# First attention of a two-layer network: scores computed once, kept in SBUF and shifted there

## The chip, the cores and the metric

The kernel runs on one core of a Trainium2 chip. Its time is the device time of one execution in microseconds (us), the median of three runs. Times of stages and instructions come from one profiled execution of the same program.

## The reference, cut to what matters

Eight batches go through two layers, each a cross attention and a feed-forward part, always on the layer-normalised sum so far. The part that the change touches is the first attention:

```python
# per batch: x 512 x 256, context 1024 x 192, 16 heads of 64
q = layernorm(x) @ w_q;  k, v = split(context @ w_kv)
scores = einsum('bhqd,bhkd->bhqk', q, k) * 64 ** -0.5
out = einsum('bhqk,bhkd->bhqd', softmax(scores), v)
x = x + out @ w_out + b_out
```

After it come, for each batch, two of eight expert networks picked by the batch's first row (`experts`), and a second attention with 16 heads of width 16 (`second_attention`). The last feed-forward part, whose inputs and hidden values are rounded to levels that depend on all eight batches, runs when everything else is done.

## The kernel before

Everything is float32, and softmax's maxima are exact. Heads go in pairs: a pair's two heads of width 64 fill the 128 rows of the array, one in each half. There are 64 pairs in all (eight batches of eight), numbered n; keys go in eight tiles of 128, numbered kt, and the 512 queries lie along the free dimension.

For pair n the first attention does the following.

- `queries(n)`, `keys(n)`: two projections, copied to SBUF by ScalarE. `values` makes the values of four heads at once.
- `maxima(n, i)`: eight score tiles laid out queries by keys are computed for the maxima alone (`sm`, L557), and VectorE reduces each straight from PSUM (`mx`, L564).
- `maxima_rows`: the 512 maxima per head are transposed to rows (`tm`, L576), split in a high and a low part by ScalarE and VectorE (`mr`, L580 and L581), and written into the tile `m_rows` by four small DMAs on SP's queue (L584).
- `scores(n, kt)` through `exponentials`: the scores are computed again, keys by queries (L595), a matmul of `m_ones` with `m_rows` subtracts the maxima within the same PSUM accumulation (L598), and ScalarE takes the exponential from PSUM to SBUF (`e`, L600). GpSimd adds the eight tiles of exponentials up (`esum`, L754 and L756).
- `attend(n, half)`: values times exponentials, in two halves of four tiles (`av`, L696). `normalise` makes the sums over keys by a matmul (`den`, L715), and GpSimd divides by Newton steps (L729 to L737). `project` multiplies by `w_out` and adds to x.

The order on TensorE is written by `weave`. It takes two generators, `first_stream` (the first attention of all batches, then the rest of the last batch) and `second_stream` (for each other batch experts, second attention, last norm), and picks the next step by a planner's account: each step carries its costs on TensorE, on one of the four PSUM slots, and on an engine. A batch's second stream can start only when its first attention is done. TensorE's queue keeps that order; the other engines' queues are ordered by the framework's own scheduler. [...] Every PSUM tile, of both streams, comes from one ring of four slots (`ps_s`), so a tile has to be drained before the fourth one after it can be written.

The weights of the first attention lie whole in SBUF (`wq`, `wkv`, `wo`), and wide tiles of both streams share one ring of 13.

Of the kernel before, what the change touches and what calls it, by code (L numbers as in the profile page):

```python
# [18 lines left out]
P = 128  # L19
# [110 lines left out]
def kernel(  # L130
# [33 lines left out]
    H = 16  # L164
# [7 lines left out]
    NF = FF // P  # L172
    assert S == 512 and D == 256 and L == 1024 and AD == 64 and CD == 16 and NE == 8
# [28 lines left out]

    fold = const.tile([P, AD], F32, name="fold")
# [17 lines left out]
    pp = attn.enter_context(tc.tile_pool(name="pp", bufs=13))  # L221
    op = attn.enter_context(tc.tile_pool(name="op", bufs=2))

    def load_ctx(b):
        raws = []
        for g in range(NK // 4):
            t = pp.tile([P, 4, DC], F32, tag="e", name=f"ctx_{b}_{g}")
            nc.sync.dma_start(
                out=t, in_=cross[b, g * 512 : (g + 1) * 512].rearrange("(t p) d -> p t d", p=P)
            )  # L230
            raws.append(t)
        return raws

    load_x(0)
    loaded = {0: load_ctx(0)}

    wq = wts.tile([P, DH, H * AD], F32, name="wq")
    nc.sync.dma_start(out=wq, in_=a_wq.rearrange("(c p) n -> p c n", p=P))

    wkv = wts.tile([P, 2, 2 * H * AD], F32, name="wkv")  # L240
    nc.sync.dma_start(out=wkv[:, 0, :], in_=a_wkv[0:P, :])
    for h in range(2):
        nc.sync.dma_start(out=wkv[h * CR : (h + 1) * CR, 1, :], in_=a_wkv[P:DC, :])
    wo = wts.tile([P, H // 2, D], F32, name="wo")
    nc.sync.dma_start(out=wo, in_=a_wo.rearrange("(h p) n -> p h n", p=P))
# [96 lines left out]
    def feed_forward_weights():  # L342

        nw, no, wT = (
            [pp.tile([P, 1024], F32, tag="e", name=f"{name}{i}") for i in range(2)]
            for name in ("nw", "no_f", "wT")
# [3 lines left out]
        for i in range(2):  # L350
            nc.sync.dma_start(
                out=no[i].rearrange("p (f n) -> p f n", n=D),
                in_=f_wo[i * 512 : (i + 1) * 512, :].rearrange("(f p) n -> p f n", p=P),
            )
        bir = small.tile([NF, P], F32, tag="bir", name="bir", bufs=1)
# [16 lines left out]
        for k, parts in enumerate((wT, no)):  # L372
# [26 lines left out]
            if k == 0:  # L399
                wi = pp.tile([P, DH, FF], BF16, tag="e", name="wi")  # L400
# [38 lines left out]
    def normed(pool, tag, b, mean, rs):  # L439
        xn = pool.tile([P, NT, D], F32, tag=tag, name=f"xn_{b}")  # L440
        for t in range(NT):
            nc.gpsimd.tensor_scalar(  # L442
                xn[:, t, :], xs[b][:, t, :], mean(t), rs(t), ALU.subtract, ALU.mult
            )
        return xn
# [18 lines left out]
    def layernorm_T(b, xT, by_place=False):  # L464
# [3 lines left out]
        def norm():  # L468
            mv, rs = norm_of(b)
            xn.append(  # L470
                normed(pp, "e", b, lambda t: mv[:, t, 0:1], lambda t: rs[:, t : t + 1])
            )
# [10 lines left out]
    def context_T(b, raws, c1, c2):  # L483

        def wide(g):
# [16 lines left out]
        for g in range(NK // 4):  # L504
            steps.append((0, [(0.5, "s", "act", 0.6, "full")], lambda g=g: wide(g)))
            steps.append((0, [(0.5, "s", "dve", 0.5, "full")], lambda g=g: narrow(g)))
# [84 lines left out]
    def exponentials(name, q, k, rows_of, kt, scale):  # L591
# [7 lines left out]
        e = pp.tile([P, 2, 512], F32, tag="e", name=f"e_{name}_{kt}")  # L599
# [6 lines left out]
    def prologue(b):  # L606

        if b in loaded:
            raws = loaded.pop(b)
        else:  # L610
            load_x(b)
            raws = load_ctx(b)
# [9 lines left out]
        return layernorm_T(b, xTs[b]) + context_T(b, raws, c1, c2), bias  # L622

    def first_attention():


        q, k, v, o, mx, es, esum, division = {}, {}, {}, {}, {}, {}, {}, {}
        last = B * NP - 1

        def queries(n):  # L630
            b, p = divmod(n, NP)
            q[n] = kvp.tile([P, S], F32, tag="q", name=f"q_{n}")
            t = bank(f"pq_{n}")
            for c in range(DH):
                nc.tensor.matmul(  # L635
                    t, wq[:, c, tok(p)], xTs[b][:, c, :], start=(c == 0), stop=(c == DH - 1)
# [3 lines left out]
        def keys(n):  # L640
            b, p = divmod(n, NP)
            c1, c2 = contexts[b]
            k[n] = kvp.tile([P, L], F32, tag="k", name=f"k_{n}")
# [6 lines left out]
                        wkv[:, 0, tok(p)],  # L650
                        c1[:, g * 512 : (g + 1) * 512],
                        wkv[g * CR : (g + 1) * CR, 1, tok(p)],
# [7 lines left out]
        def values(m, half):  # L660

            b, g = divmod(m, H // G)
            c1, c2 = contexts[b]
            if half == 0:
                v[m] = kvp.tile([P, NK, G * AD], F32, tag="v", name=f"v_{m}")
            cols = slice(H * AD + g * G * AD, H * AD + (g + 1) * G * AD)
            t = ps_s.tile([P, 2, 512], F32, tag="s", name=f"pv_{m}_{half}")
            parts = []
            for j in range(2):
                for i in range(2):  # L670
# [7 lines left out]
                            wkv[:, 0, cols],  # L678
                            c2[rows_, at],
                            wkv[rows_, 1, cols],  # L680
# [28 lines left out]
        def normalise(n, piece):  # L709


            if piece == 0:
                den = bank(f"den_{n}")
                for h in range(2):
                    nc.tensor.matmul(  # L715
                        den[h * AD : (h + 1) * AD, :],
                        ones_c,
                        esum[n][:, h, :],
# [3 lines left out]
                e = op.tile([P, S], F32, tag="rec", name=f"rec_{n}", bufs=1)  # L722
                y = op.tile([P, S], F32, tag="guess", name=f"guess_{n}", bufs=1)
                division[n] = e, y
                nc.scalar.copy(e, den)
                nc.vector.tensor_scalar(
# [720 lines left out]
```

## Time and profile before

| | |
|---|---|
| median of 3 runs (lowest, highest) | 3667.57 us (3667.2, 3667.66) |
| profiled execution | 3661.27 us, span 3659.5 us |
| TensorE busy, share of the span | 3425.3 us, 94% |
| GpSimd | 2228.9 us, 61% |
| VectorE | 1871.2 us, 51% |
| ScalarE | 1581.8 us, 43% |
| first and last cast of a pair's maxima (`mr`, L580) | 41.2 us, 3132.9 us |
| eight pairs in the steady part (casts of pairs 16 and 24) | 747.1 to 1160.9 us |

The span runs from the first to the last instruction. In the profile's lines an operation is named by its line, engine and tiles, output first; L595 is line 595 of the kernel. PE is TensorE, PEld its weight loads, DVE is VectorE, ACT is ScalarE, POOL is GpSimd, SPq the queue of the sync engine that issues the DMAs. A matmul in float32 appears as two records, and matmuls in different quarters of the array overlap, so that the steps of the chain of waits, not the mean of a record, tell what a tile costs. PEclk is the clock that TensorE was granted, 1.00 being full speed.

### The profile page before, as it was taken

Reading aid. Unit: us, or ns where it says so; the run is one execution under the profiler, and the core shown is the slowest. Engines: PE = TensorE matmul, PEld = TensorE weight load, DVE = VectorE, ACT = ScalarE, POOL = GpSimd, SP = SyncE. Lnnn points to the kernel's source line nnn. Section 1 sums busy time; section 2 is a strip of 40 time slices with the busy share of each in tenths; the row PEclk is TensorE's granted clock in tenths of the full one; section 3 lists DMA queues with packets and bytes.
Section 4 is the critical chain, followed back from the end, with each engine's and each line's share of the span. In section 5 each row is a group of like instructions: output and inputs, shape, how many; then the busy total and the mean of one; then the engine's idle time right before and its main releaser. Section 6 shows DMA issues by size and latency. Waiting matters only on the chain.

```text
span 3659.5 us, 45327 instructions
## 1 busy us (share of the span) xinstructions
PE 3425.3 (94%) x17437; PEld 1636.1 (45%) x17445; DVE 1871.2 (51%) x2327; ACT 1581.8 (43%) x1871; POOL 2228.9 (61%) x1900
## 2 busy tenths in 40 slices
PE   8999999999999999999999999999999999787777
PEld 4444444444444444444444444444444444343336
DVE  4333465544654465544654465544654444355578
ACT  2333244443544344443544344443544334334467
POOL 3888845686556854687556854687456866720012
PEclk9999999999999999999999999999999999998889
DMA  3000110001110111001110010001100000021122
GB/s 103 12 15 1 32 26 20 18 27 27 27 27 1 32 30 27 19 21 29 31 27 1 27 36 21 24 13 33 28 21 15 27 23 13 11 57 38 27 75 75
DMA packets 69395, 102.27 MB, mean 28 GB/s; under 512 B 16815, under 2 KB 48316, under 8 KB 68796
## 3 DMA queue, kind: packets, MB, share of 16 engines
q1 hardware_dynamic: 69180, 99.37, 9.9%
q8 instruction: 139, 2.28, 0.3%
q14 instruction: 76, 0.62, 0.1%
HBM read 37.98 MB, written 9.96 MB: 13 GB/s over the span
## 4 chain that ended last, share of the span: by engine, by line
PE 75%; POOL 11%; DVE 8%; ACT 2%; issue 2%; SPq 1%; DMA 1%; POOLq 0%; ACTq 0%; DVEq 0%
PE av L696 11%; PE s L595 10%; PE sm L557 10%; PE cav L1062 5%; PE acc L519 4%; DVE cmx L564 3%; PE pq L635 3%; PE s_c L595 3%; PE pk L545 3%; POOL esum L756 3%; PE pv L545 3%; PE s L598 3%; POOL xn L442 2%; PE s_c L598 2%; PE sm_c L557 2%
## 5 line engine op out<-in xcount | busy, mean ns | idle before, releaser
L564 DVE TENSOR_REDUCE mx<-sm 128x2 f32<-128x1024 f32 x512 | 626.8, 1225 | 652.5 <-PE sm L557 650.6
L756 POOL TENSOR_TENSOR esum<-esum,e 128x1024 f32<-128x1024 f32 x384 | 905.7, 2358 | 33.5 <-ACT e L600 15.5
L600 ACT ACTIVATE e<-s 128x1024 f32<-128x1024 f32 x512 | 523.5, 1026 | 498.4 <-PE s L598 493.6
L564 DVE TENSOR_REDUCE cmx<-sm_c 128x2 f32<-128x1024 f32 x512 | 607.4, 1217 | 235.1 <-PE sm_c L557 234.5
L754 POOL TENSOR_TENSOR esum<-e,e 128x1024 f32<-128x1024 f32 x64 | 151.2, 2363 | 869.6 <-PE den L715 826.9
L600 ACT ACTIVATE e_c<-s_c 128x1024 f32<-128x1024 f32 x512 | 509.3, 1024 | 276.2 <-PE s_c L598 264.8
L595 PE MATMUL s<-q,k 64*128 64x512 f32 x2048 | 551.4, 615 | 17.9 <-DVE cmx L564 7.2
L557 PE MATMUL sm<-k,q 64*128 64x512 f32 x2048 | 529.8, 595 | 6.0 <-DVE cmx L564 1.9
L696 PE MATMUL av<-e,v 128*64 128x512 f32 x2048 | 467.4, 598 | 0.2 <-ACT k L658 0.2
L598 PE MATMUL s<-m_rows,m_ones 64*128 64x512 f32 x1024 | 414.0, 802 | 0.0
L736 POOL TENSOR_SCALAR guess<-rec 128x512 f32<-128x512 f32 x192 | 286.5, 1492 | 16.6
L595 PE MATMUL s_c<-cq,ck 64*128 64x512 f32 x1024 | 284.1, 548 | 9.5 <-ACT e_c L600 6.3
L595 PEld LDWEIGHTS s<-q,k 64*128 64x128 f32 x2048 | 182.4, 188 | 226.0 <-issue 153.0
L557 PE MATMUL sm_c<-ck,cq 64*128 64x512 f32 x1024 | 221.9, 435 | 57.5 <-DMA ck<-ckl 32.7
L557 PEld LDWEIGHTS sm<-k,q 64*128 64x128 f32 x2048 | 197.6, 188 | 157.3 <-issue 80.1
L696 PEld LDWEIGHTS av<-e,v 128*64 128x64 f32 x2048 | 136.2, 136 | 270.9 <-issue 257.4
L737 POOL TENSOR_TENSOR o<-o,guess 128x512 f32<-128x512 f32 x192 | 244.3, 1273 | 11.1
L684 ACT COPY v<-pv 128x1024 f32<-128x1024 f32 x64 | 64.8, 1013 | 427.3 <-PE pv L547 427.3
L1062 PE MATMUL cav<-e_c,cv 128*32 128x512 f32 x1792 | 218.0, 604 | 0.4 <-ACT e_c L600 0.4
L598 PE MATMUL s_c<-m_rows,m_ones 64*128 64x512 f32 x1024 | 210.4, 401 | 2.9 <-DMA m_rows<-mr_c 2.7
L420 POOL TENSOR_SCALAR ve<-mv 128x4 f32<-128x4 f32 x32 | 7.3, 228 | 297.9 <-DVE mv L418 293.0
L595 PEld LDWEIGHTS s_c<-cq,ck 64*128 64x128 f32 x1024 | 100.4, 190 | 189.5 <-issue 99.5
(219 smaller groups left out, 4317.9 us busy)
## 6 DMA issues: line engine op xcount, KB each, us to landing
cq<-cqs SPq DMA_DIRECT2D x256, 64.0 KB
ck<-ckh SPq DMA_DIRECT2D x128, 128.0 KB
ck<-ckl SPq DMA_DIRECT2D x128, 128.0 KB
w<-in_L_ffn_W_dram SPq DMA_DIRECT2D x32, 256.0 KB
x<-xd SPq DMA_DIRECT2D x16, 512.0 KB
ctx<-in_ctx_dram SPq DMA_DIRECT2D x16, 384.0 KB
x<-in_x_dram SPq DMA_DIRECT2D x8, 512.0 KB
m_rows<-mr SPq DMA_DIRECT2D x256, 2.0 KB
```

The lines of the kernel that those rows point to most:

```text
L545: nc.tensor.matmul(out, lhs, rhs, start=first, stop=False, skip_group_check=True)
L557: nc.tensor.matmul(s[:, h, :], q[half, tok(i)], k[half, g * 512 : (g + 1) * 512], start=True, stop=True,)
L564: nc.vector.tensor_reduce(mx[:, :, i, g], s, AX.X, ALU.max)
L595: nc.tensor.matmul(s[:, h, :], k[half, tok(kt)], q[half, :], start=True, stop=False)
L598: nc.tensor.matmul(s[:, h, :], m_ones[half, :], rows_of[half, :], start=False, stop=True)
L600: nc.scalar.activation(e, s, AF.Exp, scale=scale)
L696: nc.tensor.matmul(av[h * AD : (h + 1) * AD, :], v[m][:, kt, (at + h) * AD : (at + h + 1) * AD], es[n, kt][:, h, :], start=(kt == kts[0]), ...
L736: nc.gpsimd.tensor_scalar(y, e, 1.0, None, ALU.add)
L737: nc.gpsimd.tensor_tensor(o[n], o[n], y, ALU.mult)
L754: nc.gpsimd.tensor_tensor(esum[n], es[n, 0], es[n, 1], ALU.add)
L756: nc.gpsimd.tensor_tensor(esum[n], esum[n], es[n, kt], ALU.add)
L1062: nc.tensor.matmul(av[col : col + SL, :], va[:, v : v + SL], es[p, kt][:, h, :], start=(i == 0), stop=(i == NK // 4 - 1),)
```

## The change

Scores are computed once, keys by queries, and copied to SBUF without the maxima subtracted. VectorE keeps a running maximum over the eight tiles; eight transposes by TensorE and one reduction turn it into the maxima per query. These are spread over all partitions by one pair of matmuls, and added (with a minus sign) to the score tiles in SBUF, two tiles of a pair by VectorE from PSUM, six by GpSimd from a copy. ScalarE then takes the exponential in place. Scores of pair n + 1 are made while pair n is exponentiated. The division is a reciprocal of 256 columns on VectorE, spread by matmuls, and one product on VectorE. The first attention's weights are loaded four heads at a time, and the wide tiles have rings of their own: 12 for the first attention's scores, 5 for the second's exponentials, 3 and 1 for others. `q`, `k` and `v` of the first attention have one buffer each.

```diff
+    RINGS = {"e": 12, "ec": 5, "t": 3, "p": 1}
...
+    def load_weights(m, keys=("q", "kv", "o")):
+        g = m % (H // G)
+        cols = slice(g * G * AD, (g + 1) * G * AD)
+        if "q" in keys:
+            t = wts.tile([P, DH, G * AD], F32, tag="wq", name=f"wq_{m}")
+            nc.sync.dma_start(out=t, in_=a_wq[:, cols].rearrange("(c p) n -> p c n", p=P))
+            weights["q"] = t
...
+        def sums(n):
+            den = bank(f"den_{n}")
+            for h in range(2):
+                for g in range(NT):
                     nc.tensor.matmul(
+                        den[32 * g : 32 * (g + 1), tok(h)],
+                        ones[:, 0:32],
+                        esum[n][:, h, tok(g)],
                         start=True,
                         stop=True,
                     )
+            rec[n] = op.tile([P, 2, P], F32, tag="rec", name=f"rec_{n}", bufs=1)
+            nc.vector.reciprocal(rec[n].rearrange("p h n -> p (h n)"), den[:, : 2 * P])
+
+        def normalise(n):
+            t = bank(f"rb_{n}")
+            for g in range(NT):
+                for h in range(2):
+                    nc.tensor.matmul(
+                        t[h * AD : (h + 1) * AD, tok(g)],
+                        pick[:, g, :],
+                        rec[n][:, h, :],
+                        start=True,
+                        stop=True,
+                    )
+            nc.vector.tensor_tensor(o[n], t, o[n], ALU.mult)
...
         def scores(n, kt):
+            s = ps_s.tile([P, 2, 512], F32, tag="s", name=f"s_{n}_{kt}")
+            for h in range(2):
+                half = slice(h * AD, (h + 1) * AD)
+                nc.tensor.matmul(
+                    s[:, h, :], k[n][half, tok(kt)], q[n][half, :], start=True, stop=True
+                )
+            es[n, kt] = wide("e", [P, 2, 512], f"e_{n}_{kt}")
+            nc.scalar.copy(es[n, kt], s)
+            if kt == 1:
+                run[n] = pp.tile([P, 2, 512], F32, tag="wide", name=f"run_{n}", bufs=2)
+                nc.vector.tensor_tensor(run[n], s, es[n, 0], ALU.max)
+            elif kt > 1:
+                nc.vector.tensor_tensor(run[n], s, run[n], ALU.max)
+
+        def maxima(n):
+            t = ps_s.tile([P, 2, NT, P], F32, tag="s", name=f"trun_{n}")
+            for h in range(2):
+                for i in range(NT):
+                    nc.tensor.transpose(t[:, h, i, :], run[n][:, h, tok(i)], ident)
+            m = small.tile([P, 2, NT], F32, tag="m", name=f"m_{n}", bufs=2)
+            nc.vector.tensor_reduce(m, t, AX.X, ALU.max)
+            return m
+
+        def subtract(n, kt):
+            if kt < 2:
+                nc.vector.tensor_tensor(es[n, kt], mb[n][0], es[n, kt], ALU.add)
+            else:
+                nc.gpsimd.tensor_tensor(es[n, kt], mb[n][1], es[n, kt], ALU.add)
+
+        def spread(n):
+            t = ps_s.tile([P, 2, 512], F32, tag="s", name=f"mb_{n}")
+            for h in range(2):
+                half = slice(h * AD, (h + 1) * AD)
+                nc.tensor.matmul(
+                    t[:, h, :], m_ones[half, :], m_rows[0][half, :], start=True, stop=True
+                )
+            u = pp.tile([P, 2, 512], F32, tag="wide", name=f"mbs_{n}", bufs=2)
+            mb[n] = t, u
+            nc.scalar.copy(u, t)
+            for kt in range(4):
+                subtract(n, kt)
+
+        def exponentiate(n, kt):
+            nc.scalar.activation(es[n, kt], es[n, kt], AF.Exp, scale=AD**-0.5)
...
+            yield 0, SPREAD
+            spread(n)
+            for kt in range(2):
+                exponentiate(n, kt)
             for kt in range(NK):
...
+                    scores(n + 1, kt)
+                if kt + 2 < NK:
+                    exponentiate(n, kt + 2)
+                if kt == 0 and n > 0:
+                    yield 0, SUMS
+                    sums(n - 1)
+                add_up(n, kt)
+                if 1 <= kt <= 4:
+                    subtract(n, kt + 3)
+                if kt == 2 and n > 0:
+                    yield 0, NORM
+                    normalise(n - 1)
+                if kt == 3:
                     yield 0, HALF[0]
                     attend(n, 0)
...
+            yield 0, HALF[1]
+            attend(n, 1)
             if n < last:
+                yield 0, TURN
+                mm = maxima(n + 1)
             if n + 2 <= last:
+                yield from both(n + 2)
             if n < last:
+                yield 0, ROWS
+                maxima_rows(f"{n + 1}", mm, m_rows[0])
             if p % 2 == 0 and n > 0:
                 yield 0, OUT
                 project(n // 2 - 1)
+                load_weights(n // 2, ("o",))
...
+            if p % 2 == 1 and n < last:
+                yield from both_values(n // 2 + 1)
+                if n + 3 <= last:
+                    load_weights(n // 2 + 2, ("q", "kv"))
```

`queries`, `keys`, `values`, `attend`, `maxima_rows` and the second stream's arithmetic stay as they are; `add_up` is the former sum over the eight tiles, on GpSimd as before.

## The prediction, on record before the run

> **What bounds the kernel now.** I read the page's busy times first, then its slices, then a table of stretches.
>
> ```profile
> PE 3425.3 (94%) x17437; PEld 1636.1 (45%) x17445; DVE 1871.2 (51%) x2327; ACT 1581.8 (43%) x1871; POOL 2228.9 (61%) x1900
> ...
> PE   8999999999999999999999999999999999787777
> ...
> PEclk9999999999999999999999999999999999998889
> ```
> ```profile
> 1561.00:1948.00 387.00, 376.28 (x1925) 174.26 (x1922) 201.37 (x246) 169.85 (x199) 262.29 (x224) 1.00 0.10 26
> 3190.00:3440.00 250.00, 194.56 (x1061) 96.08 (x1061) 142.24 (x194) 105.75 (x122) 30.04 (x68) 0.87 0.17 43
> ```
>
> TensorE is busy 97% of a steady stretch at full clock; nothing else is above 68%. The second line is the stage after the first attention: busy 78%, granted clock 0.87. Then come the groups that the change touches, and rows that price new work:
>
> ```profile
> L564 DVE TENSOR_REDUCE mx<-sm 128x2 f32<-128x1024 f32 x512 | 626.8, 1225 | 652.5 <-PE sm L557 650.6
> L756 POOL TENSOR_TENSOR esum<-esum,e 128x1024 f32<-128x1024 f32 x384 | 905.7, 2358 | 33.5 <-ACT e L600 15.5
> L600 ACT ACTIVATE e<-s 128x1024 f32<-128x1024 f32 x512 | 523.5, 1026 | 498.4 <-PE s L598 493.6
> L754 POOL TENSOR_TENSOR esum<-e,e 128x1024 f32<-128x1024 f32 x64 | 151.2, 2363 | 869.6 <-PE den L715 826.9
> L1370 ACT ACTIVATE h<-h,unround 128x1024 f32<-128x1024 f32 x32 | 35.6, 1137 | 8.4 <-DVE h L1367 8.4
> L1086 DVE RECIPROCAL crec<-co 128x16 f32<-128x16 f32 x32 | 8.1, 253 | 1.0
> ```
> ```profile
> 1564.38 0.89 PE s L595 x4
> 1565.50 0.86 PE sm L557 x4
> ...
> 1582.19 1.85 PE cav L1062 x16
> ...
> 1599.63 3.43 PE av L696 x16
> ...
> 1634.83 1.02 PE txn L451 x8
> ```
>
> The last fence is from the chain of waits: a score tile costs TensorE 0.86 us, the maxima matmuls 0.23 (the step between 0.89 and the next start), half an attend 3.5. GpSimd waits for `den` 827 us in all, 13 a pair: it is off the path before. The second stream has the rest of TensorE, about 14.7 us a pair.
>
> The time of a pair is read from the starts of ScalarE's 64 `mr` casts in the timeline: 41.2 for pair 0, 418.6 for 10, 747.1 for 16, 1160.9 for 24, 2819.7 for 56, 3132.9 for 63. Eight steady pairs take 414 us.
>
> **The change, part by part, for one pair.** TensorE loses eight maxima tiles (8 x 0.86) and eight maxima matmuls (8 x 0.23): 8.7. It gains eight transposes (1.0, the `txn` row), one spread pair (0.23) and the second half of the division (8 small matmuls; between 0.4 if they overlap as `av` does and 2; I take 1.0). Net -6.5, or 416 us over 64 pairs if TensorE stayed the bound.
>
> ScalarE gains eight copies and a spread (9 x 1.01) and loses one copy of `den` (0.59); its exponentials now read SBUF (between the 1026 of `e` and the 1137 of L1370: take 1.1, +0.6 a pair). About +9.1, 583 us in all. VectorE loses eight reductions (9.8), the guess (0.69) and a small one; it gains seven maxima, a reduction and two subtractions (10 x 1.225, with a PSUM operand like `x<-acc,x` below), a product (0.69) and a reciprocal of 256 columns at 1.7 (253 ns for 16 columns against 196 for eight: 6 to 7 ns each; bounds 0.7 and 1.9): +4. GpSimd loses 13.6 of Newton steps and gains six subtractions at 2.36: about even. Per eight pairs: TensorE 331 by the rows in the new order, all other engines under 80% of that. No engine is full; the question is the chain.
>
> **The chain that is new.** In the built order TensorE's `mb(n)` is followed by scores of n+1, `av` first half, more scores, `av` second half, `trun`, projections, `tm`, and then `mb(n+1)`. Counting from `mb(n)`: the copy to SBUF ends at 1.35. GpSimd's queue has five subtractions, one sum and the sixth subtraction (for some pairs six in a row): 7 x 2.4 = 16.8, to 18.2. ScalarE's queue has the last exponential ahead of the copy that frees `av`'s slot: 19.3, then 19.9. Score tile 7 stands four slots behind `av`, so it runs at 20 to 20.9; the second half waits for tile 4's copy, 21 to 24.6; transposes to 25.6; the two projections to 30.3, then `tm`; `mr` waits behind the key copy in ScalarE's queue, 31.5. Four DMA issues take 2.7 (the timeline: 41.53 to 44.2), landing about 2 more (estimate; the nearest row is 2.56 of `ck`, 128 KB). So `mb(n+1)` stands at 36.3, although TensorE has only 26 to 28 us of first-stream work in it.
>
> I then walked eight steady pairs (16 to 23) through the built queues, with these rows, four PSUM slots and the static orders:
>
> - 16: 40.4, 17: 38 (TensorE's own sum 33 and 29): the chain, nearly alone.
> - 18: 51 (sum 41): expert matmuls wait for PSUM slots that ScalarE frees only behind the last exponential, at 19.9.
> - 19: 75 (sum 51). GpSimd's queue puts the expert bias, two layer norms and residual adds (4.9 for `xn`, 14 small steps of 0.28, 2.9 per add) between the sums of 18 and the subtractions of 19: these start 10 us late. ScalarE's queue has all eight exponentials of 19 ahead of the first copy of 20, so three slots stay full until 26.7 and TensorE stands.
> - 20: 63.6 (sum 50): ScalarE alone is full for 20 us, its exponentials of both streams and copies in line.
> - 21: 50.5, 22: 62.5, 23: 47.5 (sums 41, 50, 37): the same, and the wait for `m_rows`.
>
> Sum 428.5, against 414 before. The batch loses what TensorE saves because second-stream work lies unevenly: in pairs 0 to 9 and two of every eight there is almost none.
>
> Totals: pairs 0 to 9, 10 x 36.5 + 7 for the quantisation work on VectorE = 372 against 377, -5. Pairs 10 to 15, the walk of 18 to 23, 350 against 328.5, +22. Five batches +70 (428.5 against 414.5). Pairs 56 to 62, little second stream, 279 against 313, -34. The tail has the same 107 second-attention tiles left in both orders; the last `den` now waits for thirteen GpSimd steps, +5. Together +58.
>
> **The clock.** The row 3190 to 3440 says 78% busy, clock 0.87; before's steady rows 97% and 1.00. The changed batch has 331 of TensorE work in 428: 77%. The Trainium skill (TensorE: Matmul & The Clock Gate, Part 1, "What's actually happening") speaks against this change: the array falls to half clock after an idle window of about 3.4 us and needs as much work to come back. The chain leaves waits of 4 to 6 us in most pairs. By the row at 0.87, TensorE's 331 become 380, half of the extra on the path: +25 a batch, +200 in all. By 1.00, nothing. I take half, +100, since the waits beside second-stream work are shorter than in that row.
>
> A second rule that I weigh: GPSIMD Engine Reference, 1. Specifications, has the SBUF interface shared with VectorE when VectorE reads two SBUF tensors or runs a two-port mode. The rows show both sides:
>
> ```profile
> L1088 DVE TENSOR_TENSOR ca<-co,crec x32: 424/1857/2578, 518.0 to 3481.2; 128x256 f32<-128x256 f32 x32
> ...
> L529 DVE TENSOR_TENSOR x<-acc,x x32: 1223/1225/1226, 153.6 to 3209.9; 128x1024 f32<-128x1024 f32 x32
> ```
>
> `ca` reads SBUF twice and is held up to 2.6 us; `x<-acc,x` has a PSUM operand and is not. Every new VectorE operation of the pair (maxima, reduction, subtractions, product) has an operand in PSUM. So 1.225 stands by the row; by the rule read widely, nine of them would pay the 1.4 that `ca` pays at its median, 13 us a pair on VectorE, which I leave out.
>
> Costed at nothing: the weight loads (four DMAs each 0.6 of SP's queue per two pairs; in the built order they stand behind the `m_rows` DMAs or wait for matmuls already done; 0 to +77 if they land ahead); one buffer of `q`, `k`, `v` (written after the last score tile anyway); the second stream's ring of five (its sixth tile waits for `cav`, 0 to 1.2 a pair, under its own slot wait).
>
> Sum: 3661.3 + 58 + 100 = 3819 for a profiled execution; the median of the runs stood 6.3 above it: 3825, say 3820.
>
> **Rivals.**
>
> 1. Faster: the chain stays hidden. It decides at 414 for eight pairs. If slot waits in ScalarE's line are shorter than I walked, each pair costs the larger of TensorE's sum and the 36.3 of the chain: 36, 38, 42, 51, 50, 41, 53, 41, together 351, and the total is 3661 - 6 x 63 - 39, about 3240; halfway to my walk, 3480. For it: TensorE's freed 6.5 a pair, and no engine over 80%. Against: before, TensorE's sum by the same rows was 385 and took 414, although nothing but TensorE was on the path.
> 2. Much slower: the clock at 0.87 or less throughout and 1 us more per pair for some 15 hand-overs: 3661 + 58 + 200 + 64 = 3983. For it the row of 3190 to 3440.
> 3. The change does not take place as told: excluded, the built order has six subtractions on GpSimd and two on VectorE in each pair, and no second score tile.
>
> **How the numbers follow.** Chain-bound at a partly lowered clock, 0.52: 3700 to 3920, likeliest 3820. Much slower, 0.25. Faster, 0.20, around 3480, of which half lies above 3560. Within 0.2% (about what a measurement of this kernel can tell from no change, 7 us) 0.03. So slower 0.77. The range 3570 to 3990 leaves out 0.1 at the faster end and 0.1 above.
>
> **What would show it.** Right: TensorE busy share near 80% in the steady stretch with PEclk at 8 or 9; ScalarE about 2170 us busy, VectorE about 2130, GpSimd about the same as before; pairs without second-stream work 36 us apart; `e` copies and `av` among the waits for slots; GpSimd's subtractions in the chain of waits. Wrong: eight steady pairs under 414 us with GpSimd absent from the chain, or simple pairs near 28 us, which would mean that subtractions start before I think or cost less than 2.36.

## The result and the profile after

The changed kernel takes 3914.27 us, median of four runs (3911.32 to 3917.03), against 3667.53 us before: 1.0673 times as long, 95% interval 1.0654 to 1.0691. Its profiled span is 3913.2 us against 3659.5, 254 us more.

From the page of the changed kernel: busy times, then TensorE's slices and its clock, then the groups of the new chain (columns: tiles, count, busy us and mean ns, idle us just before and what ended most of it).

```profile
PE 3213.4 (82%) x16797; PEld 1527.1 (39%) x16805; DVE 2113.7 (54%) x2459; ACT 2051.0 (52%) x2383; POOL 2270.1 (58%) x1580
...
PE   6777778888788879888788889888888888868787
...
PEclk9888889999899989999899989998999999989888
...
L822 POOL TENSOR_TENSOR e<-mbs,e 128x1024 f32<-128x1024 f32 x384 | 896.6, 2366 | 1089.0 <-ACT mbs L834 1089.0
...
L839 ACT ACTIVATE e<-e 128x1024 f32<-128x1024 f32 x512 | 531.1, 1057 | 350.0 <-POOL e L822 323.1
L806 DVE TENSOR_TENSOR run<-s,run 128x1024 f32<-128x1024 f32 x384 | 469.5, 1223 | 428.0 <-ACT e L801 412.4
...
L801 ACT COPY e<-s 128x1024 f32<-128x1024 f32 x512 | 505.0, 1014 | 182.1 <-PE s L797 158.8
```

TensorE is 212 us less busy than before and the kernel 254 us longer, with every other engine below 60%. GpSimd waits 1089 us for the spread (17 a pair): it can't start earlier. The exponentials wait 323 us for its subtractions. VectorE's maximum (L806) waits 412 us for ScalarE's copy of the same tile. The page's chain of waits reaches back over the last stage alone (4% of the span), so the chain of a pair is read from the timeline.

The chain in a pair without second-stream work (start, length, engine, operation, idle time before). The kernel is the one without the rounding steps (below), in which pair 2 is undisturbed:

```profile
125.29 0.59 PE L829 MATMUL mb<-m_rows,m_ones 64*128 64x512 f32 x2
...
126.66 1.02 ACT L834 COPY mbs<-mb 128x1024 f32<-128x1024 f32 x1
...
127.75 11.65 POOL L822 TENSOR_TENSOR e<-mbs,e 128x1024 f32<-128x1024 f32 x5 [7.98 <-ACT mbs L834]
...
141.66 2.34 POOL L822 TENSOR_TENSOR e<-mbs,e 128x1024 f32<-128x1024 f32 x1
...
144.04 1.06 ACT L839 ACTIVATE e<-e 128x1024 f32<-128x1024 f32 x1 [3.55 <-POOL e L822]
145.00 0.57 ACT L749 COPY o<-av 128x512 f32<-128x512 f32 x1
145.47 2.84 ACT L801 COPY e<-s 128x1024 f32<-128x1024 f32 x3
...
145.62 1.66 PE L797 MATMUL s<-q,k 64*128 64x512 f32 x4 [3.64 <-ACT o L749]
...
147.79 4.48 PE L740 MATMUL av<-e,v 128*64 128x512 f32 x16 [0.52 <-DVE run L806]
...
152.21 1.09 PE L812 MATMUL trun<-ident,run 128*128 128x128 f32 x8
...
158.78 0.25 ACT L619 CAST mr<-tm 8x128 fp32r<-8x128 f32 x1
```

Counted from the start of the spread (`mb`), the last subtraction ends at 18.7, the last exponential at 19.8, the copy `o` that frees the eighth tile's slot at 20.3, and the rows of the next maximum are cast at 33.5. The prediction had 18.2, 19.3, 19.9 and 31.5.

Times by stage, from the starts of ScalarE's `mr` casts, in us (in brackets the prediction's difference, its +100 for the clock not placed in any stage):

| stage | before | after | difference | without subtraction |
|---|---|---|---|---|
| to pair 0 | 41.2 | 47.0 | +6 (0) | 48.8 |
| pairs 0 to 9 | 377.4 | 422.3 | +45 (-5) | 341.1 |
| pairs 10 to 15 | 328.5 | 375.5 | +47 (+22) | 323.7 |
| pairs 16 to 55 | 2072.6 | 2219.4 | +147 (+70) | 1990.1 |
| pairs 56 to 62 | 313.2 | 330.6 | +17 (-34) | 279.3 |
| the rest | 526.6 | 518.4 | -8 (+5) | 500.2 |

### The profile page after: what moved, and what is told of

Its sections match the earlier page's. It is cut to its first block, busy times and chain, and to the rows that moved or that the text cites. A ratio compares the mean times of both kernels' runs of the same rounds, so it can differ in the third digit from the quotient of the medians.

```text
span 3913.2 us, 44834 instructions
## 1 busy us (share of the span) xinstructions
PE 3213.4 (82%) x16797; PEld 1527.1 (39%) x16805; DVE 2113.7 (54%) x2459; ACT 2051.0 (52%) x2383; POOL 2270.1 (58%) x1580
## 5 line engine op out<-in xcount | busy, mean ns | idle before, releaser
L822 POOL TENSOR_TENSOR e<-mbs,e 128x1024 f32<-128x1024 f32 x384 | 896.6, 2366 | 1089.0 <-ACT mbs L834 1089.0
L797 PE MATMUL s<-q,k 64*128 64x512 f32 x2048 | 597.3, 684 | 160.2 <-ACT o L749 89.8
L839 ACT ACTIVATE e<-e 128x1024 f32<-128x1024 f32 x512 | 531.1, 1057 | 350.0 <-POOL e L822 323.1
L806 DVE TENSOR_TENSOR run<-s,run 128x1024 f32<-128x1024 f32 x384 | 469.5, 1223 | 428.0 <-ACT e L801 412.4
L801 ACT COPY e<-s 128x1024 f32<-128x1024 f32 x512 | 505.0, 1014 | 182.1 <-PE s L797 158.8
L740 PE MATMUL av<-e,v 128*64 128x512 f32 x2048 | 516.5, 649 | 61.6 <-DVE run L806 28.5
L634 PE MATMUL s_c<-cq,ck 64*128 64x512 f32 x1024 | 276.5, 530 | 44.6 <-ACT e_c L639 11.2
L820 DVE TENSOR_TENSOR e<-mb,e 128x1024 f32<-128x1024 f32 x128 | 150.8, 1220 | 174.6 <-ACT mbs L834 174.0
L596 PEld LDWEIGHTS sm_c<-ck,cq 64*128 64x128 f32 x1024 | 109.9, 205 | 235.3 <-ACT e L801 72.4
L804 DVE TENSOR_TENSOR run<-s,e 128x1024 f32<-128x1024 f32 x64 | 78.3, 1224 | 200.6 <-ACT e L801 200.6
L699 ACT COPY k<-pk 128x1024 f32<-128x1024 f32 x64 | 64.8, 1013 | 185.7 <-PE pk L586 185.7
```

Of the source, the lines that this page charges most:

```text
L596: nc.tensor.matmul(s[:, h, :], q[half, tok(i)], k[half, g * 512 : (g + 1) * 512], start=True, stop=True,)
L634: nc.tensor.matmul(s[:, h, :], k[half, tok(kt)], q[half, :], start=True, stop=False)
L740: nc.tensor.matmul(av[h * AD : (h + 1) * AD, :], v[m][:, kt, (at + h) * AD : (at + h + 1) * AD], es[n, kt][:, h, :], start=(kt == kts[0]), ...
L797: nc.tensor.matmul(s[:, h, :], k[n][half, tok(kt)], q[n][half, :], start=True, stop=True)
L801: nc.scalar.copy(es[n, kt], s)
L806: nc.vector.tensor_tensor(run[n], s, run[n], ALU.max)
```

## The experiments

Each diff is against the changed kernel unless it says otherwise; ratios are to the kernel before, run beside it on the same chip.

### Without the subtraction, and without the copies too

```diff
         def subtract(n, kt):
-            if kt < 2:
...
+            return
```

> The changed kernel without the eight subtractions of the maximum (that part of the computation is left out; the exponentials read the copied scores as they are); everything else, the maxima, their rows, the spread and its copy too, stays. Theory 1, the chain through GpSimd's six subtractions sets the pair: the last exponential no longer stands at 19.3 us after the spread, so pairs without second-stream work fall from 36 to 45 us to about 29 (TensorE's own sum), eight steady pairs to 350 to 390, the whole to 3350 to 3500 us. Theory 2, ScalarE's line of copies and exponentials holds the PSUM slots whatever GpSimd does: ScalarE has the same work, simple pairs stay above 34, the whole at 3750 or more.

3486.63 us, ratio 0.9512 (0.9496 to 0.9528). The whole is as theory 1 has it, and so are the pairs without second-stream work or rounding (0, 2, 4, 5, 7 and 8: 29.2 to 31.2); eight steady pairs take 396 to 399, above its 390. The 428 us less are the price of subtracting in SBUF: the eight subtractions of a pair, six of them on GpSimd, and the wait of the exponentials for the maximum, since without the subtraction no exponential needs the spread.

```diff
 # on top of it
-            nc.scalar.copy(es[n, kt], s)
+            nc.scalar.activation(es[n, kt], s, AF.Exp, scale=AD**-0.5)
...
         def exponentiate(n, kt):
+            return
```

> The kernel without subtractions (3487 us), in which also the eight copies of scores to SBUF are left out: ScalarE takes the exponentials straight from PSUM (so the maxima, though still taken and spread, are not subtracted), and VectorE copies the first tile of the maximum. ScalarE does 8 x 1.01 less a pair. Theory 2 as a second part (ScalarE's line of copies and exponentials, and PSUM slots behind it, is what lies between the 396 us of eight steady pairs there and TensorE's own sum of 331): eight pairs 345 to 370, the whole 3150 to 3320 us. Rival (what is left there is TensorE at a lowered clock, second-stream waits and DMAs): within 60 us of 3487.

3419.14 us, ratio 0.9329 (0.9313 to 0.9344): 67 less than the kernel before it, just outside the rival's 60 and far from theory 2. Once nothing is subtracted, the copies on ScalarE hold up little.

The two divide the change. Without both it is 3667 - 3419 = 248 us faster than the kernel before: that is the worth of computing scores once, and with it of the new division, the weight loads, the new order and the subtraction that TensorE no longer does; these were not taken apart. The copies to SBUF take back 67 and the subtractions there 428. The stretch of eight steady pairs (24 to 31) shows where. In these lines (start:end, length, then busy us of PE, PEld, DVE, ACT and POOL, TensorE's clock, DMA share, GB/s) the kernels are before, after, without subtraction, and without both:

```profile
1160.90:1576.40 415.50, 404.42 (x2062) 188.38 (x2060) 215.53 (x263) 179.69 (x212) 274.38 (x233) 1.00 0.09 24
```
```profile
1288.80:1732.90 444.10, 373.56 (x1982) 175.28 (x1981) 239.81 (x279) 237.79 (x276) 279.50 (x192) 0.93 0.12 32
```
```profile
1109.90:1509.10 399.20, 363.80 (x1982) 172.61 (x1981) 219.24 (x263) 240.46 (x276) 169.03 (x144) 0.97 0.13 35
```
```profile
1075.80:1465.30 389.50, 361.38 (x1982) 171.21 (x1981) 228.29 (x271) 177.41 (x212) 168.51 (x144) 0.97 0.13 36
```

TensorE stands 11 us of the stretch before, 71 after, 35 without subtraction and 28 without both. The same matmuls take 10 us more at the clock of 0.93 than at 0.97. Subtracting in SBUF costs the stretch 35 us of waiting and 10 of TensorE's time at the lower clock.

### Who subtracts: four and four, or all on VectorE

```diff
-            if kt < 2:
+            if kt < 4:
```

> The changed kernel with four subtractions on VectorE (from PSUM) and four on GpSimd, in place of two and six. Theory 1 (chain through GpSimd): in the built order GpSimd then has four steps between the spread's copy and the last subtraction where it had seven, 7.1 us less; VectorE has 2.4 more beside it. Pairs without second-stream work fall by about 7, the others by half of that: 3590 to 3740 us. Theory 2 (ScalarE's line and the PSUM slots behind it): within 60 us of 3914.

3811.99 us, ratio 1.0403 (1.0386 to 1.042): 102 less than the changed kernel, on theory 1's side, but short of the 174 that it gave at least. A simple pair such as 7 falls from 37.6 to 33.4, not by 7; eight steady pairs only from 444 to 438. With GpSimd's part shorter, something else ends last; the next run shows one such thing.

```diff
-            if kt < 2:
...
+            nc.vector.tensor_tensor(es[n, kt], mb[n], es[n, kt], ALU.add)
...
-            u = pp.tile([P, 2, 512], F32, tag="wide", name=f"mbs_{n}", bufs=2)
-            mb[n] = t, u
-            nc.scalar.copy(u, t)
+            mb[n] = t
```

> The changed kernel with all eight subtractions on VectorE, straight from the spread tile in PSUM; the copy of the spread to SBUF goes, GpSimd has only its sums, and TensorE's order stays as it is. Theory 1 (it is GpSimd's 2.37 us a step, one behind the other and behind GpSimd's other work, that lengthens the pair, not the subtraction as such): eight steps of 1.22 on VectorE are quicker than ScalarE's line of an exponential and a copy for each (2.07), so the exponentials wait only for the first; pairs without second-stream work near 31 us, eight steady pairs 400 to 415, the whole 3510 to 3650 us, below the kernel before. Rival (VectorE's line becomes the bound: 7.3 us more a pair, ahead of the maxima that the next score tiles' slots wait for): no better than the even split, 3780 us or more.

3728.32 us, ratio 1.0173 (1.0156 to 1.019): the best variant of the changed kernel that computes everything, 186 less than the changed kernel, still 1.7% above the one before. Both expectations missed. With GpSimd out of the chain a simple pair takes 33.5 (pair 7), not 31, and eight steady pairs 430, not 400 to 415. The timeline of pair 8 (VectorE, then ScalarE) shows VectorE's queue in the chain instead:

```profile
345.20 4.62 DVE L819 TENSOR_TENSOR e<-mb,e 128x1024 f32<-128x1024 f32 x4 [4.83 <-PE mb L826]
349.73 1.74 DVE L767 RECIPROCAL rec<-den 128x256 f32<-128x256 f32 x1
351.40 1.16 DVE L804 TENSOR_TENSOR run<-s,e 128x1024 f32<-128x1024 f32 x1
352.48 1.21 DVE L819 TENSOR_TENSOR e<-mb,e 128x1024 f32<-128x1024 f32 x1
353.60 1.21 DVE L806 TENSOR_TENSOR run<-s,run 128x1024 f32<-128x1024 f32 x1
```
```profile
359.19 0.59 ACT L749 COPY o<-av 128x512 f32<-128x512 f32 x1 [2.15 <-PE av L740]
```

Four subtractions and the reciprocal stand ahead of the first maximum, which must be taken before a score tile's slot is free; the attend's first half gets a slot late and ScalarE, next in line with that half's copy, stands 2.15 us. So of the 428 us, 186 came from putting the work on GpSimd, with the copy of the spread that GpSimd needs (65 us of ScalarE, off here too). The other 242 stay when VectorE does it all, at 67% busy in the steady stretch (289.16 of 430.20); the wait for the maximum is among them.

### The rounding of the feed-forward weights

```diff
-                rounded(of(parts, f), s_w[k][:, f : f + 1], -128.0, 127.0)
+                pass
```

> The changed kernel without the 32 VectorE operations that round the feed-forward weights (the rounding is left out; all that surrounds it stays). They run in the first ten pairs, read and write SBUF alone, and took up to 2.4 us each there beside GpSimd's subtractions and sums, against 0.3 alone. Theory 3 (these held operations stand ahead of VectorE's subtractions and maxima and cost the first ten pairs most of the 45 us that they grew): the first ten pairs fall from 422 to 380 to 395, the whole to 3870 to 3890 us. Rival (they are beside the path, the first ten pairs are slow for the chain itself): the first ten pairs within 8 us of 422, the whole within 8 of 3914.

3888.94 us, ratio 1.0611 (1.0593 to 1.0629): 25 less, with the whole where theory 3 had it. The first ten pairs take 398.2, above its 395: the rounding is 24 of the 45 us that they grew. Pairs 1 and 3 fall from 47.6 and 51.3 to 37.2 and 39.3, and no other pair moves by more than 1.7. The reason stands in VectorE's timeline of pair 1 in the changed kernel:

```profile
88.30 0.56 DVE L367 TENSOR_SCALAR wT<-wT,s_w 128x256 f32<-128x256 f32 x2
...
91.81 4.77 DVE L368 TENSOR_SCALAR wT<-wT 128x256 f32<-128x256 f32 x2
96.51 4.77 DVE L367 TENSOR_SCALAR wT<-wT,s_w 128x256 f32<-128x256 f32 x2
101.20 2.34 DVE L820 TENSOR_TENSOR e<-mb,e 128x1024 f32<-128x1024 f32 x2
```

Two such operations take 0.56 us while GpSimd is idle and 4.77 once it subtracts: each takes as long as one step of GpSimd's (2.37), and the first two exponentials' subtractions stand behind them. GpSimd's sums do the same: without the subtraction two of these operations still take up to 4.91, and pair 1 takes 47.8. The kernel before had a smaller bulge in the same pairs (41.3 and 37.2 against 32.1 in pairs 0 and 2), though there these operations take 0.28 to 0.47 us each.

### TensorE's order between the maximum and the spread

Projections first:

```diff
+            if n + 2 <= last:
+                yield from both(n + 2)
             yield 0, HALF[1]
             attend(n, 1)
...
                 mm = maxima(n + 1)
-            if n + 2 <= last:
-                yield from both(n + 2)
```

> The changed kernel with the two projections for pair n+2 ahead of the second half of the attend and of the transposes of the maximum, so that they are out of the way between the transposes and the rows of the maximum. Theory 1 (chain): the 4.65 us that they stand in the chain come off where TensorE waits anyway for the seventh score tile's slot or for the last exponentials: 3 to 4.6 us a pair in some 26 pairs, less in the others, 3680 to 3810 us. Theory 2 (PSUM slots behind ScalarE's line are what is short): two more tiles ahead of the same slots give nothing, 3880 to 3960 us.

3962.93 us, ratio 1.081 (1.0792 to 1.0828), 49 more. Neither theory (the second ended at 3960); my expectation had overlooked the order of the queue. The projections can't stand ahead of the eighth score tile, since `q` and `k` have one buffer that this tile still reads; so they only go from behind the second half of the attend to ahead of it, and the row's transpose now waits for the reduction in the open:

```profile
169.02 0.27 PE L615 MATMUL tm<-ident,m 128*8 128x128 f32 x1 [2.12 <-DVE m L814]
```

The way from the transposes to the spread did get shorter, 8.9 us on average instead of 13.5, but the attend ahead of it comes later by the projections, and the first ten pairs take 422.9, as in the changed kernel. The loss lies in pairs with second-stream work, and there the edit moved that work too: `weave` plans from the order of the steps, and between its spread and the next one, pair 18 has 104 matmul records of the second stream where it had 56. It takes 72.3 instead of 49.8. What the order costs and what the new plan costs was not separated.

Rows first:

```diff
                 mm = maxima(n + 1)
+                yield 0, ROWS
+                maxima_rows(f"{n + 1}", mm, m_rows[0])
             if n + 2 <= last:
                 yield from both(n + 2)
-            if n < last:
-                yield 0, ROWS
-                maxima_rows(f"{n + 1}", mm, m_rows[0])
```

> The changed kernel with the transpose and the DMAs of the maximum's rows (tm, mr, four DMAs) ahead of the two projections for pair n+2; the projections then lie beside the DMAs. Theory 1 (the chain from one spread to the next): the 4.65 us of the projections come off the chain, and TensorE waits some 1.3 for the reduction of the transposed maximum instead: pairs without second-stream work fall by 3 to 3.5 us, in all 26 to 64 times that, 3690 to 3840 us. Theory 2 (PSUM slots behind ScalarE's line decide, the rows come early enough anyway): within 30 us of 3914.

3980.99 us, ratio 1.0857 (1.0838 to 1.0877), 67 more, outside both. TensorE takes its queue in order, and the spread stands behind projections and value tiles there, so the rows come early and wait: for pair 8 it is 10.4 us from `tm` to `mb`. From the transposes to the spread it is now 14.9 us on average instead of 13.5: the same work, and the wait for the reduction (1.32 in the first line). In pairs 16 to 23 the second stream stays where it was.

```profile
393.55 0.27 PE L615 MATMUL tm<-ident,m 128*8 128x128 f32 x1 [1.32 <-DVE m L814]
...
403.94 0.59 PE L829 MATMUL mb<-m_rows,m_ones 64*128 64x512 f32 x2
```

Spread ahead of the value tiles:

```diff
             yield 0, SPREAD
             spread(n)
+            if p % 2 == 0 and n > 0:
+                yield from both_values(n // 2)
...
-            if p % 2 == 1 and n < last:
-                yield from both_values(n // 2 + 1)
# and queries, rows, keys in this order behind the transposes
```

> The changed kernel with another order between the transposes of the maximum and the next spread, nothing added or left out: query projection, then tm, mr and the DMAs, then the key projection, then the spread of pair n+1, and only then the two value tiles, which so lie beside the subtractions. In the kernels with early projections and with rows first TensorE's in-order queue had the same work between the transposes and the spread as before, and lost 1.3 to 2.1 us more to a wait for the reduction. Theory 4 (that work in TensorE's own queue is part of the chain, wherever it stands between trun and mb): from trun to mb 12.0 us (two projections, two value tiles) become about 6.5 in odd pairs and 9.6 about 6.5 in even ones; in some 27 pairs all of it, in the others half: 3680 to 3810 us. Rival (subtractions and PSUM slots alone set the pair, an earlier spread only lengthens the wait for the eighth score tile's slot): within 40 us of 3914.

3967.86 us, ratio 1.0827 (1.0809 to 1.0845), 54 more, outside both. Theory 4 holds where there is little second-stream work: the first ten pairs take 394.2 instead of 422.3, pair 25 takes 34.8 instead of 41.3. Where there is, it loses more: pairs 26, 29 and 30 grow by about 8 each. Timeline of pair 10, ScalarE and then TensorE:

```profile
453.93 2.00 ACT L839 ACTIVATE e<-e 128x1024 f32<-128x1024 f32 x2 [6.83 <-POOL e L822]
455.84 0.99 ACT L728 COPY v<-pv 128x1024 f32<-128x1024 f32 x1
```
```profile
451.72 1.13 PE L586 MATMUL pv<-wkv,c 64*128 64x256 f32 x8
457.37 0.20 PE L1014 MATMUL route<-wr,xT 128*1 128x8 f32 x2 [4.52 <-ACT xT L492]
```

The copies that free the value tiles' slots now stand behind exponentials that wait 6.83 us for subtractions. The copy `xT`, which TensorE's next step (`route`) needs, stands behind them in ScalarE's queue, and TensorE waits 4.52. The plan of the second stream changed here as well: pair 22 has 230 of its records instead of 202 and takes 84.6 instead of 76.7. But pair 21, with 81 instead of 109, grew too (55.9 instead of 48.2), so the plan isn't the whole of it.

The even split and this order together:

> Both orders together: four subtractions on each of VectorE and GpSimd, and the spread ahead of the value tiles and behind the key projection. If the chain is one line with both in it (theories 1 and 4), the gains add: 102 us of the even split and what the spread's place gives, 3560 to 3720 us. If they share one cover (ScalarE's line, 18 us of copies and exponentials a pair, becomes what ends last): no more than the better of the two, 3780 to 3815.

3821.29 us, ratio 1.0428 (1.0411 to 1.0445): no better than the even split alone (3812), and just above the 3815 that I gave for a shared cover. The first ten pairs do gain again (375.3 instead of 393.8), and pairs 16 to 55 lose it (2202.7 instead of 2187.7).

### The copy that frees the eighth tile's slot

```diff
-                nc.scalar.copy(o[n], av)
+                nc.vector.tensor_copy(o[n], av)
```

> The changed kernel with the copy of the first half of the attend to SBUF on VectorE in place of ScalarE, where it stands behind the last exponential of the pair. Theory 2 (PSUM slots behind ScalarE's line): the eighth score tile no longer waits for the last exponential; it runs some 3.6 to 6 us earlier and at full clock, the second half of the attend about 2 us earlier (it still needs the last exponential): 2 to 3 us in some 26 to 64 pairs, 3730 to 3860 us. Theory 1 alone (the last exponential behind GpSimd's subtractions sets the second half, whatever slot the score tile has): within 30 us of 3914.

3910.88 us, ratio 1.0665 (1.0645 to 1.0684): no change, as the second theory had it. The eighth tile now runs at once, but the second half of the attend needs the slot behind it, and that is held by a score tile whose copy stands behind the last exponential too, which this half needs in any case; TensorE waits in one place instead of the other:

```profile
366.00 3.70 PE L797 MATMUL s<-q,k 64*128 64x512 f32 x16
374.16 5.05 PE L740 MATMUL av<-e,v 128*64 128x512 f32 x16 [4.46 <-DVE run L806]
```

### The clock, and the division

```diff
                     scores(n + 1, kt)
+                    if kt == 6 and (n < 9 or n % 8 in (0, 1) or n >= 56):
+                        fill(n)   # 8 matmuls into av_n's second bank
```

> The changed kernel with eight more matmuls (a result that nobody reads, into the unused bank of av's slot) behind the seventh score tile of the next pair, in the 27 or so pairs with little second-stream work; there TensorE stood 3.6 to 6 us for the slot of the eighth tile, and the eighth tile and the second half of the attend took 1.7 to 2.1 and 4.5 to 5.5 us instead of 0.9 and 3.6. Theory 3 (these are the clock's price for the wait): with TensorE at work in the wait they go back to 0.9 and 3.6, 1.5 to 3 us in each of these pairs, 3830 to 3875 us. Rival (they are long for what they wait for, or the added matmuls end late): 3905 us or more.

4072.7 us, ratio 1.1108 (1.1088 to 1.1128), 158 more, and it tells nothing of the clock. The added matmuls waited for ScalarE's copy of the same tile's other bank (3.65 us in pair 4), so they didn't fill the wait; they came behind it:

```profile
262.22 8.78 PE L758 MATMUL av<-e,ident 128*64 128x512 f32 x16 [3.65 <-ACT o L750]
```

The kernel before with the new division alone:

```diff
-                nc.scalar.copy(e, den)
...
+                nc.vector.reciprocal(r.rearrange("p h n -> p (h n)"), den[:, : 2 * P])
...
+                nc.vector.tensor_tensor(o[n], t, o[n], ALU.mult)
```

> The kernel before with only the new division: den spread over 128 partitions by sixteen matmuls, a reciprocal of 256 columns on VectorE, and sixteen matmuls with pick, in place of ScalarE's copy, VectorE's guess and GpSimd's Newton steps. By the prediction's sum TensorE gains about 1.0 us a pair (0.4 to 2) in a kernel that TensorE bounds, and GpSimd's freed 13.6 give nothing: 3690 to 3790 us, likeliest 3730. Rival (VectorE's 1.75 us of reciprocal and the wait of rb for it stand in TensorE's line too): 3800 us or more.

3692.13 us, ratio 1.0068 (1.005 to 1.0086): 26 us, or 0.4 us a pair, the lower end of what I gave.

## Why the prediction was right, and where its steps were off

The forecast was 3820 us and 3914 was measured: 247 more than before where I had 153, at the upper end of the case that I held likeliest (3700 to 3920). By stage the five steady batches came near (147 more, where the walk's 70 and half of the clock's 25 a batch make 132). The surplus stands at both ends: 50 us in the first ten pairs and 51 in pairs 56 to 62.

- **The mechanism holds where a pair has little else.** There the chain from one spread to the next sets the pair, and it goes through GpSimd's steps, ScalarE's line and the PSUM slots. Without subtraction the kernel is faster than before; with all of it on VectorE it lies between. Without the rounding, pairs 0 to 3, 5, 7 and 8 take 36.6 to 39.3 (pair 4 40.6) where I had 36.5. In a steady stretch TensorE is busy 84% at clock 0.93, where I had near 80% and a clock of 8 or 9 tenths.
- **The walk of pairs 16 to 23** had 40.4, 38, 51, 75, 63.6, 50.5, 62.5, 47.5; measured 44.2, 41.4, 49.8, 73.2, 67.2, 48.2, 76.7, 43.1. Seven are within 5 us, with signs both ways. The sum is 428.5, or 441 with half of the 25 us a batch that I had for the clock; measured 444. Pair by pair that is closer than the walk deserves, since it had no clock in it. Pair 22 is 14 too short. It isn't the subtraction: without any, the same pair still takes 73.4, without the copies too 73.0. TensorE alone is busy 64 us in it, where my sum of its rows was 50 (cut from spread to spread, while the measured interval has two value tiles more at its start, about 5 us). My 331 us of TensorE work in eight pairs was low as well: 361 at clock 0.97 without subtraction and copies. In the first rival, the eight terms add up to 352, and those of pairs 17, 22 and 23 (38, 53, 41) are more than the larger of 36.3 and the walk's sums (29, 50, 37); no step of the forecast rests on it.
- **The first ten pairs** were the worst step: +45 instead of -5. It took ten simple pairs and 7 us of rounding. The rounding cost 24 of it, and the granted clock in that stretch is 0.87 against 0.98 before; pair 6 carries the next batch's prologue (49.8; 46.4 before), and in its timeline two transposed tiles stand in the wait for the slot, and the context's second load, into a ring of one, is waited for:

```profile
325.05 1.11 PE L483 MATMUL txn<-ident,xn 128*128 128x128 f32 x4 [4.17 <-ACT o L749]
...
335.48 1.09 PE L526 MATMUL tc<-ident,ctx 128*128 128x128 f32 x4 [3.44 <-DMA ctx<-in_ctx_dram]
```

  In pair 9 (44.6) layer-norm steps of 0.2 us stand between GpSimd's subtractions, and the wait for the slot is 6.69.
- **Pairs 56 to 62**: +17 instead of -34. "Little second stream" was wrong: pairs 58 and 59 take 53.8 and 60.8. My 279 is what the stage takes without subtraction (279.3), by coincidence.
- **The clock**: I took +100 on the path. TensorE is busy 3213.4 us after and 3082.0 without subtraction for the same matmuls (16797 and 16805 records), 131 more, at a mean granted clock of 0.915 against 0.958. The trace's record of the clock has full and half speed alone; TensorE is busy at half speed for 468 us after, 221 without subtraction and 115 before. If work takes twice as long then, the lowered clock makes TensorE busy 124 us longer than without subtraction, near the 131, and 176 longer than before (estimates, half of each difference). How much of that lies on the path no run separates. The rows show the clock at work. After a wait of 1.74 us the eighth tile takes 1.13 and the attend 3.65, at a granted clock of 1.00. After 3.64 they take 1.66 and 4.48 (above), at 0.64 and 0.81. After 6.09, in pair 25 of the changed kernel, they take 2.08 and 5.54, at 0.61 over both. That agrees with the rule of the Trainium skill that the prediction weighed (TensorE: Matmul & The Clock Gate, Part 1, "What's actually happening"): the two waits above 3.4 us were followed by a lowered clock, the one of 1.74 was not.

```profile
412.02 1.13 PE L797 MATMUL s<-q,k 64*128 64x512 f32 x4 [1.74 <-ACT o L749]
414.19 3.65 PE L740 MATMUL av<-e,v 128*64 128x512 f32 x16 [1.04 <-DVE run L806]
```
```profile
1359.20 2.08 PE L797 MATMUL s<-q,k 64*128 64x512 f32 x4 [6.09 <-ACT o L749]
...
1361.37 5.54 PE L740 MATMUL av<-e,v 128*64 128x512 f32 x16
```
```profile
411.90:417.90 6.00, 4.78 (x20) 1.36 (x20) 4.68 (x4) 3.82 (x5) 5.76 (x4) 1.00 0.00 0
1359.10:1366.95 7.85, 7.66 (x21) 2.13 (x22) 4.90 (x4) 3.80 (x5) 7.49 (x10) 0.61 0.01 2
```

  The last fence has the stretches of these two cases; the third number from the right is the granted clock.

- **The shared SBUF interface**: right for the new operations, since `run` takes 1223 ns throughout; but the same rule (GPSIMD Engine Reference, 1. Specifications) bears on VectorE work that was there already, the rounding: it took up to 2.4 us where it takes 0.28 beside an idle GpSimd, and I had charged it 7 in all. The rounding has one tensor in, so the rule would need it to run in a two-port mode, and no run here shows that.
- **Engines' busy times**: GpSimd 2270 (same, as told), VectorE 2114 (2130), ScalarE 2051 (2170). The exponential from SBUF takes 1.057 where I had 1.1, 22 us in all. For the rest, ScalarE's instructions by their own durations grew from 1630 us to 2194, 564 where I had 583; the page counts the time in which one overlaps the next once.
- **At nothing**: no wait in the trace names a weight load (`wq`, `wkv`, `wo`); the kernel without reloads was not run. No wait of the projections names the single buffer of `q` and `k` either, but that buffer is what forbids earlier projections.

What stays open: the clock's price on the path, since the filler didn't fill; how the 242 us that VectorE's subtractions still cost divide between the wait for the maximum, its queue and the slots; what the new plan of the second stream cost in the runs with another order; and why the parts before pair 0 and after pair 63 came out 6 us longer and 8 shorter.

## What to carry to other kernels

When the bound engine is relieved by handing a step to others, walk the new dependence from one iteration's start to the next before counting busy time: here 59 us of new waiting in a stretch of eight pairs outweighed 31 us of TensorE's work saved. A queue that is taken in order turns one late operation into held slots: here, moving a wait (a copy to another engine, a spread ahead of values) leads to the next slot that stands behind the same late exponential. The TensorE that hardly waited (11 us) also kept its clock at 1.00 in that stretch, and the one that waited 71 had 0.93, so a change that makes it wait pays twice.

## What the runs showed that was not expected

- A VectorE operation that reads and writes SBUF alone (128x256, 0.28 us) took up to 2.4 us beside GpSimd's adds, one whole step of GpSimd's. The 32 of them took 40.4 us in all (10.6 in the kernel before), and without them the kernel is 25 us faster.
- VectorE's maximum over a score tile and ScalarE's copy of the same tile never overlapped: `run` (L806) waited 412 us for copies that it doesn't read from. The program orders them so: all 384 records of L806 wait for one semaphore, and ScalarE's instructions alone count it up. A program without that wait was not run.
- A write to one bank of a two-bank PSUM tile waited for a read of its other bank (the filler, 3.65 us). Here too it is the program: weight loads of the filler (22 of 410) wait for ScalarE's semaphore.
- An order that shortens most pairs without second-stream work by 3 to 8 us made the whole 54 us slower, with the second stream's plan changed along with it.
